# Last feed-forward: three passes of an exact product in one PSUM bank, raised in place by ScalarE

## The chip, the cores and the metric

The kernel runs on one core of one Trainium2 chip. A core has a matrix engine (TensorE, "PE" in the profile, with its weight loads as "PEld"), VectorE ("DVE"), ScalarE ("ACT") and GpSimd ("POOL"), which run side by side, each through its own list of instructions in order, and wait for each other by semaphores. TensorE writes only into PSUM, a small memory of 8 banks of 128 partitions x 512 float32; VectorE and ScalarE read results from there. The metric is the device time of one execution in microseconds (us). Before the change it is 470.54 us, the median of 3 runs (470.39 to 470.64).

## The reference

Two transformer-like layers follow each other over `x` of shape 2 x 512 x 512 (batch, rows, features), each with an attention and a feed-forward part, and a layer norm behind each of the four. Only the last attention and the last feed-forward matter here:

```python
qkv = jnp.einsum('bsc,cf->bsf', x, Wqkv) + bqkv      # head width 128
attn = jax.nn.softmax(jnp.einsum('bqd,bkd->bqk', q, k) * scale, axis=-1)
out = jnp.einsum('bqk,bkd->bqd', attn, v)
x = _layernorm(x + jnp.einsum('bqd,dc->bqc', out, Wo) + bo)
...
gate = jnp.einsum('bsh,ih->bsi', x, w_gate)          # 1376 hidden units
up = jnp.einsum('bsh,ih->bsi', x, w_up)
inter = jax.nn.silu(gate) * up
x = _layernorm(x + jnp.einsum('bsi,hi->bsh', inter, w_down))
```

All of it is float32, and the feed-forward has to be near to exact float32.

## The kernel before

**An exact product out of three fast passes.** TensorE multiplies two float32 operands in several internal passes, but operands of the narrower type `float32r` in one. The last feed-forward therefore splits each operand into parts whose single-pass products add up to the float32 product. `row_parts` (L820) makes of a block of rows an upper part h (ScalarE, L803), a rest l (VectorE, L824) and a difference d = h - 4096 l (VectorE, L825). `weight_parts` (L812) makes of a block of weights h (ScalarE, L803), a copy multiplied by 4096 called `big` (ScalarE, L809), l = big - 4096 h (VectorE, L817) and d = l - h (VectorE, L818). The products h·h and l·l go to one PSUM bank `pm` ("main"), d·d to another, `pc` ("cross"). The result is (1 + 1/4096)·pm + pc/4096. `sum_up` (L1116) makes it: ScalarE copies pc times 1/4096 to SBUF (L1120), then VectorE adds pm times (1 + 1/4096) to it (L1121).

**Tiling.** The 1376 hidden units are cut into 11 chunks of 128 (the last has 96), which are taken in the order `turn`; j counts them. A step is a pair (b, j) of a batch and a chunk. `up1` (L1144) computes for a step gate and up (a = 0 and 1), each with 3 x 4 matmuls of 128 x 128 by 128 x 512, the cross pass first; then come `sum_up` for gate, SiLU on ScalarE (L1163), `sum_up` for up, and their product on VectorE (L1165). The first chunk (j = 0) runs differently: gate and up side by side, and block by block of the 512 features in the order h, l, d, so that it can start while the row parts are still being made. The chunk of 96 has a form of its own (`up1_joined`, L1124), in which half of up is packed behind gate. The steps run (0,0), (0,1), (0,2), (1,0), (1,1), (1,2), then j = 3 to 8 for both batches in turn, then (0,9), (0,10), (1,9), (1,10). Behind step (0,1) the rows of batch 1 are transposed on TensorE (L1042) and split.

**The down products.** `down1` (L1188) handles one tile of 128 rows: 11 cross matmuls into `pdc`, 22 main matmuls into `pdm`, and two additions on VectorE (L1205) that multiply each bank by its factor and add it to `x`; then statistics (L1208, L1214), 1/standard deviation on GpSimd (L145, L146), an offset on GpSimd (L1000), the scaling on ScalarE (`scalar_norm`, L1001) and the store. There are 8 tiles; the last is cut into two halves of 256 columns, each with its own banks, and its norm is finished by VectorE and ScalarE together (L1220 to L1226).

**What sets the order.** The kernel is written in program order; a scheduler orders the instructions of TensorE, VectorE and ScalarE from it, GpSimd's stay as written, and `issue_after` in the source ties some. Splitting weights for later chunks (`split_up`, `split_down`) has no PE work of its own, and the scheduler puts it where the engines seem to have room. Space for the parts comes from a list `free` of SBUF pieces that are done with; an instruction that writes into a reused piece waits for its last reader.

**Ahead of it, the end of the attention.** For batch 1: `values` (L982) multiplies by the probabilities in two halves of 256 columns (L989); VectorE copies each half out of PSUM (L993), `output` (L1003) multiplies it by `wo1` (L1005), `attended` (L1008) adds it to `x` on VectorE (L1010). Rows of batch 0 are scaled by ScalarE (L1001) and transposed by TensorE (L1042); rows of batch 1 get statistics (L137, L139), GpSimd's L145 and L146, and are scaled by VectorE (L151).

Of the kernel before, what the change touches and what calls it, by code (L numbers as in the profile page):

```python
# [10 lines left out]
F32 = mybir.dt.float32  # L11
# [8 lines left out]
P = 128  # L20
# [18 lines left out]
def kernel(  # L39
# [754 lines left out]

    BIG = 4096.0
    MAIN, CROSS = 1.0 + 1.0 / BIG, 1.0 / BIG
    UPPER = 1.0 - 2.0**-13
    cutp = ctx.enter_context(tc.tile_pool(name="cutp", bufs=2))  # L800

    def upper(h, src):
        return nc.scalar.activation(h, src, AF.Copy, scale=UPPER)  # L803

    def weight_upper(w, h, name):

        upper(h, w)
        big = cutp.tile([P, 512], F32, tag="big", name=f"big_{name}")
        nc.scalar.activation(big, w, AF.Copy, scale=BIG)  # L809
        return big  # L810

    def weight_parts(w, parts, name, big=None):  # L812

        h, l, d = parts
        if big is None:
            big = weight_upper(w, h, name)
        nc.vector.scalar_tensor_tensor(l, h.bitcast(F32), -BIG, big, ALU.mult, ALU.add)  # L817
        return nc.vector.tensor_sub(d, l.bitcast(F32), h.bitcast(F32))  # L818

    def row_parts(src, parts):  # L820

# [18 lines left out]
        del free[:n]  # L840
        return got

    def split_up(j, room, bigs=(None, None)):

        c = turn[j]
        n = CHUNKS[c][1]
        for a in range(2):
            up_parts[j, a] = room[3 * a : 3 * a + 3]
            if n == P:
                w = gus[c][:, a].rearrange("p k i -> p (k i)")  # L850
            else:
                w = gus[c][a]
            if n == P or a == 0:
                done = weight_parts(w, up_parts[j, a], f"gu{j}_{a}", bigs[a])
                continue

            u, w = (v.rearrange("p (k i) -> p k i", k=NK) for v in (up_parts[j, a][0], w))
            h = u[:, :, : P // 2]
            upper(h, w)
            done = nc.vector.tensor_sub(u[:, :, P // 2 :], w, h.bitcast(F32))  # L860
        own = wffn.tile([P, 2 * n // P, 512], F32R, tag=f"gu{c}", name=f"ugu_{c}")
        free.extend(units(own))
        return done
# [49 lines left out]

    room2 = room1[6:] + take(4)
    with tc.issue_after(moved.ins):
        bigs2 = [
            weight_upper(
                gus[turn[2]][:, a].rearrange("p k i -> p (k i)"), room2[3 * a], f"gu2_{a}"
            )
            for a in range(2)  # L920
        ]

    probs = []

# [46 lines left out]
    moved = exponentials(1, got1, {1: copies[-4], 2: copies[-2]})  # L971
    table(AF.Silu, moved)
    with tc.issue_after(scaled_max.ins):
        done = split_up(2, room2, bigs2)
    with tc.issue_after(done.ins):
        for _, sums in probs:
            nc.vector.reciprocal(sums, sums)
# [106 lines left out]

    evicted = [fp.tile([P, S], F32, tag="sg", name=f"ev_{i}") for i in range(2)]
    for i in range(2):
        evicted += units(query_tile(f"ev_q{i}"))

    def products(b, j, a):


        h, l, d = (u.rearrange("p (k i) -> p k i", k=NK) for u in up_parts[j, a])
        pc, pm = psum(f"pc_{b}_{j}_{a}"), psum(f"pm_{b}_{j}_{a}")
        passes = [
            [(w[:, k], x3[b][k][i], (pm, pm, pc)[i]) for i, w in enumerate((h, l, d))]
            for k in range(NK)
        ]
        return pc, pm, passes

    def run(passes, by_block):  # L1100

        if by_block:
            todo = [p for block in passes for p in block]
        else:
            todo = [block[i] for i in (2, 0, 1) for block in passes]
        begun = {}
        for _, _, p in todo:
            begun[id(p)] = begun.get(id(p), 0) + 1
        left = dict(begun)
        for w, x, p in todo:  # L1110
            nc.tensor.matmul(  # L1111
                p, w, x, start=(left[id(p)] == begun[id(p)]), stop=(left[id(p)] == 1)
            )
            left[id(p)] -= 1

    def sum_up(pc, pm):  # L1116

        ev = evicted.pop(0)
        evicted.append(ev)
        nc.scalar.activation(ev, pc, AF.Copy, scale=CROSS)  # L1120
        nc.vector.scalar_tensor_tensor(ev, pm, MAIN, ev, ALU.mult, ALU.add)  # L1121
        return ev

    def up1_joined(b, j, it):  # L1124

        n = CHUNKS[turn[j]][1]
        pc, pm, passes = products(b, j, 0)
        run(passes, False)
        u = up_parts[j, 1][0].rearrange("p (k i) -> p k i", k=NK)
        p = psum(f"pm_{b}_{j}_1")  # L1130
        run([[(u[:, k], x3[b][k][i], p) for i in range(2)] for k in range(NK)], True)
        both = sum_up(pc, pm)
        moved = nc.scalar.activation(both[:n], both[:n], AF.Silu)
        wide = evicted.pop(0)
        evicted.append(wide)
        nc.scalar.copy(wide[: P // 2], p[P // 2 :])
        nc.scalar.copy(wide[P // 2 : n], both[n:])
        nc.vector.tensor_add(wide[: P // 2], wide[: P // 2], p[: P // 2])
        nc.vector.tensor_mul(it, both[:n], wide[:n])
        return moved  # L1140

    its = {}

    def up1(b, j):  # L1144

        n = CHUNKS[turn[j]][1]
        g = j // 4
        if (b, g) not in its:
            its[b, g] = fp.tile(
                [P, GROUPS[g], S], F32, tag=f"it{b}{g}", name=f"it_f1{b}{g}", bufs=1  # L1150
            )
            if g == turn.index(last) // 4:
                nc.gpsimd.memset(its[b, g][96:, turn.index(last) % 4, :], 0.0)
        if n < P:
            return up1_joined(b, j, its[b, g][:n, j % 4, :])
        (pc0, pm0, passes0), (pc1, pm1, passes1) = (products(b, j, a) for a in range(2))
        if j == 0:
            run([[x for y in zip(p, q) for x in y] for p, q in zip(passes0, passes1)], True)
        else:
            run(passes0, False)  # L1160
            run(passes1, False)
        gate = sum_up(pc0, pm0)
        moved = nc.scalar.activation(gate, gate, AF.Silu)  # L1163
        wide = sum_up(pc1, pm1)
        nc.vector.tensor_mul(its[b, g][:n, j % 4, :], gate, wide)  # L1165
        return moved

    down_parts = []

    def split_down():  # L1170
        c = turn[len(down_parts)]
        parts = take(3)
        weight_parts(wds[c], parts, f"wd{c}")
        down_parts.append(parts)
        free.append(wdp.tile([P, 512], F32R, tag=f"wd{c}", name=f"uwd_{c}"))

# [8 lines left out]
            got.append((room, parts))  # L1185
        return got

    def down1(b, t, got, cuts):  # L1188

        x = xs[b][t]  # L1190
        w = HID // cuts
        st = small.tile([P, cuts, 6], F32, tag=f"st{cuts}", name=f"st_{b}_{t}")
        for i in range(cuts):
            cols = slice(i * w, (i + 1) * w)
            pc, pm = psum(f"pdc_{b}_{t}_{i}"), psum(f"pdm_{b}_{t}_{i}")
            for p, kinds in ((pc, (2,)), (pm, (0, 1))):
                for j in range(len(turn)):
                    for kind in kinds:
                        nc.tensor.matmul(  # L1199
                            p[:, :w], got[j // 4][1][kind][:, j % 4], down_parts[j][kind][:, cols],  # L1200
                            start=(j == 0 and kind == kinds[0]),
                            stop=(j == last and kind == kinds[-1]),
                        )
            for p, f in ((pc, CROSS), (pm, MAIN)):
                nc.vector.scalar_tensor_tensor(  # L1205
                    x[:, cols], p[:, :w], f, x[:, cols], ALU.mult, ALU.add
                )
            nc.vector.bn_stats(st[:, i, :], x[:, cols])  # L1208
            if i == 0 and cuts > 1:

# [17 lines left out]
            free.extend(room)  # L1228

    free.extend(units(const.tile([P, 3, 512], F32R, tag="wqkv", name="u_wqkv")))  # L1230
    for tag in ("wo1", "bo"):
        free.append(const.tile([P, 512], F32R, tag=tag, name=f"u_{tag}"))

# [1 line left out]
    steps += [(b, j) for j in range(3, last - 1) for b in range(B)]  # L1235
    steps += [(0, last - 1), (0, last), (1, last - 1), (1, last)]
    ahead = 3
    for i, (b, j) in enumerate(steps):
        before, moved = moved, up1(b, j)
        if i == 1:  # L1240
            rooms[1] = rows_room(1, "r1")
            x3[1], _ = split_rows(1, rooms[1])
        if b == 1 and j not in (0, 1, 3, 6):

            kept = 2 if j == 2 else 0
            free.extend((up_parts[j, 0] + up_parts[j, 1])[kept:])
        if (b, j) == (0, last):
            free.extend(rooms[0])
        if (b, j) == (1, last):
            free.extend(rooms[1])  # L1250
        with tc.issue_after(before.ins):
            if ahead <= last and b == 1:
                split_up(
                    ahead, room0 if ahead in (3, 6) else take(6 if turn[ahead] < last else 4)
                )
# [6 lines left out]

    while len(down_parts) <= last:
        split_down()
    quarters.append(split_tile(0, 1))
    for i, (b, t) in enumerate(order):
        down1(b, t, quarters[i], 2 if i == len(order) - 1 else 1)
        if i + 2 < len(order):
            quarters.append(split_tile(*order[i + 2]))


# [49 lines left out]
```

## Time and profile before

| | |
|---|---|
| median of 3 runs | 470.54 us |
| span of the profiled execution, first to last instruction | 468.7 us |
| mean granted clock of TensorE | 0.998 |
| VectorE, whole span | 329.5 us in 627 instructions |
| ScalarE, whole span | 267.5 us in 507 instructions |
| GpSimd, whole span | 115.1 us in 144 instructions |
| L1120, ScalarE, pc times 1/4096 | 42 instructions, 0.59 us each |
| L1121, VectorE, pm added | 42 instructions, 0.69 us each |
| L809, ScalarE, `big` | 32 instructions, 0.62 us each |
| L1205, VectorE, down sums | 18 instructions, 0.69 us each (0.42 us for 256 columns) |

The profile shows one execution. Its page has no total for that execution, only the span; the median of the runs is 1.84 us above it, which is what lies before the first and behind the last instruction. An instruction's duration includes its latency, so that instructions of one engine overlap a little in the records; where instructions stand back to back the distance between their starts is their price.

### The profile page before, as it was taken

Reading aid. Unit: us, or ns where it says so; the run is one execution under the profiler, and the core shown is the slowest. Engines: PE = TensorE matmul, PEld = TensorE weight load, DVE = VectorE, ACT = ScalarE, POOL = GpSimd, SP = SyncE. Lnnn points to the kernel's source line nnn. Section 1 sums busy time; section 2 is a strip of 40 time slices with the busy share of each in tenths; the row PEclk is TensorE's granted clock in tenths of the full one; section 3 lists DMA queues with packets and bytes.
Section 4 is the critical chain, followed back from the end, with each engine's and each line's share of the span. In section 5 each row is a group of like instructions: output and inputs, shape, how many; then the busy total and the mean of one; then the engine's idle time right before and its main releaser. Section 6 shows DMA issues by size and latency. Waiting matters only on the chain.

```text
span 468.7 us, 5727 instructions
## 1 busy us (share of the span) xinstructions
PE 461.0 (98%) x1883; PEld 329.0 (70%) x1883; DVE 329.5 (70%) x627; ACT 267.5 (57%) x507; POOL 115.1 (25%) x144
## 2 busy tenths in 40 slices
PE   9999999999999999999999999999999999999994
PEld 8454444434478888888866567888888888888884
DVE  1165677767876767775979889895755778998632
ACT  3344799557756767456756842584645768443101
POOL 0235101566543053600357032000000000050111
PEclk9999999999999999999999999999999999999999
DMA  8989900000006500051390000000000000001001
GB/s 284 381 297 363 387 9 0 0 0 3 1 1 134 201 1 3 11 162 45 91 390 31 0 1 1 1 0 1 1 0 1 0 1 1 1 24 45 37 31 45
DMA packets 21651, 35.02 MB, mean 75 GB/s; under 512 B 9840, under 2 KB 10736, under 8 KB 21616
## 3 DMA queue, kind: packets, MB, share of 16 engines
q1 hardware_dynamic: 19616, 33.73, 20.7%
q10 hardware_dynamic: 1872, 0.56, 0.5%
q8 instruction: 22, 0.36, 0.3%
q0 software_dynamic: 128, 0.26, 0.3%
q14 instruction: 13, 0.11, 0.1%
HBM read 31.40 MB, written 2.10 MB: 71 GB/s over the span
## 4 chain that ended last, share of the span: by engine, by line
PE 71%; ACT 7%; DVE 5%; issue 3%; POOL 0%; POOLq 0%; DVEq 0%; ACTq 0%
PE pm L1111 17%; PE pg_f L611 9%; PE pu_f L611 9%; PE pc L1111 8%; PE pdm L1199 7%; PE pd_f L666 4%; PE pdc L1199 4%; DVE x L450 3%; PE pqk L893 3%; PE po L428 2%; ACT y L441 2%; ACT t L463 2%; PE pv L906 2%; PE pot L989 1%; PE po L1005 1%
## 5 line engine op out<-in xcount | busy, mean ns | idle before, releaser
L428 PE MATMUL po<-mw,q 128*128 128x512 f32 x128 | 57.1, 598 | 0.3 <-DVE mv_a L139 0.2
L352 PE MATMUL pq<-xt_a,wq 128*128 128x512 f32 (+1 forms) x152 | 56.9, 526 | 0.0
L145 POOL TENSOR_TENSOR rstd_f<-mv_f,ln_eps 128x1 f32<-128x1 f32 x15 | 4.4, 293 | 169.3 <-DVE mv_f L1214 130.2
L428 PEld LDWEIGHTS po<-mw,q 128*128 128x128 f32 x128 | 22.9, 189 | 32.1 <-issue 17.7
L352 PEld LDWEIGHTS pq<-xt_a,wq 128*128 128x128 f32 x152 | 26.2, 190 | 27.4 <-issue 25.7
L1111 PE MATMUL pm<-r,ugu 128*128 128x512 f32 x152 | 37.7, 389 | 0.0
L1111 PE MATMUL pm<-r,it_early 128*128 128x512 f32 x144 | 36.7, 392 | 0.0
L1111 PEld LDWEIGHTS pm<-r,ugu 128*128 128x128 f32 x152 | 28.5, 188 | 5.9
L1111 PEld LDWEIGHTS pm<-r,it_early 128*128 128x128 f32 x144 | 27.0, 188 | 6.1 <-issue 0.5
L169 ACT ACTIVATE ta_f<-y_f,below_half 128x512 int8<-128x512 f32 (+1 forms) x22 | 15.9, 721 | 27.0 <-DVE y_f L157 26.7
L450 DVE SCALAR_TENSOR_TENSOR x<-po,den,x 128x511 f32<-128x511 f32 x40 | 29.8, 745 | 1.9
L1121 DVE SCALAR_TENSOR_TENSOR ev_q<-pm,ev_q 128x512 f32<-128x512 f32 x27 | 18.6, 688 | 14.4 <-PE pm L1111 14.4
L637 DVE SCALAR_TENSOR_TENSOR it_f<-tb_f,ta_f 128x512 fp32r<-128x512 int16 (+1 forms) x22 | 15.4, 702 | 18.3 <-ACT tb_f L170 18.3
L445 POOL TENSOR_TENSOR y<-y,y 128x511 f32<-128x511 f32 x16 | 20.3, 1271 | 31.5 <-ACT y L441 30.8
L388 ACT ACTIVATE e<-pq,bq 128x512 f32<-128x512 f32 x16 | 11.1, 692 | 24.1 <-PE pq L352 20.6
L611 PE MATMUL pg_f<-xh,tu 128*128 128x512 f32 x88 | 24.3, 398 | 0.0
L1120 ACT ACTIVATE ev_q<-pc 128x512 f32<-128x512 f32 x27 | 16.0, 593 | 14.2 <-PE pc L1111 14.1
L465 POOL TENSOR_SCALAR td<-wd,inv_down 128x512 fp32r<-128x512 f32 x11 | 18.2, 1668 | 22.1 <-DVE inv_down L205 22.1
L611 PE MATMUL pg_f<-xl,tu 128*128 128x512 f32 x88 | 23.6, 390 | 0.0
L611 PE MATMUL pu_f<-xh,tu 128*128 128x512 f32 x88 | 23.5, 389 | 0.0
L611 PE MATMUL pu_f<-xl,tu 128*128 128x512 f32 x88 | 23.5, 389 | 0.0
L1001 ACT ACTIVATE x<-x,off_f,rstd_f 128x512 f32<-128x512 f32 x7 | 5.7, 816 | 27.7 <-POOL off_f L1000 27.7
(315 smaller groups left out, 1087.5 us busy)
## 6 DMA issues: line engine op xcount, KB each, us to landing
gu<-in_gu SPq DMA_DIRECT2D x20, 512.0 KB, 7.9
wo<-in_wo SPq DMA_DIRECT2D x16, 512.0 KB, 6.9
wd<-in_wd SPq DMA_DIRECT2D x20, 256.0 KB, 4.5
wq<-in_wq SPq DMA_DIRECT2D x8, 256.0 KB, 4.9
x<-in_x SPq DMA_DIRECT2D x7, 256.0 KB, 5.4
out<-x SPq DMA_DIRECT2D x7, 256.0 KB, 2.0
wqkv<-in_wqkv SPq DMA_DIRECT2D x1, 768.0 KB, 10.8
xt_f<-squares SPq DMA_DIRECT2D x9, 64.0 KB, 2.4
```

The costliest lines, as they stand in the source:

```text
L169: nc.scalar.activation(a[:n], y, AF.Relu, bias=below_half[:n])
L352: done = nc.tensor.matmul(pq[:, at], wq[h][:, k, :], xt[:, k, at], start=(k == 0), stop=(k == NK - 1),)
L428: nc.tensor.matmul(po, qs[b][h0 + j][:, ts(t, P)], mw[:, h0 + j, :], start=True, stop=True,)
L445: nc.gpsimd.tensor_add(ys[0][:, :LAST], ys[0][:, :LAST], y[:, :LAST])
L450: steps.append(nc.vector.scalar_tensor_tensor(x[:, :LAST], four[j][:, :LAST], d, x[:, :LAST], ALU.mult, ALU.add))
L465: eng.tensor_scalar(out, w, factor, None, ALU.mult)
L611: nc.tensor.matmul(pp[a], t[:, a, i % NK, :], x2[b][i], start=(i == 0), stop=(i == 2 * NK - 1),)
L666: nc.tensor.matmul(pd, inter[b][c][:, ts(t, P)], td[c].bitcast(F32R), start=(c == 0), stop=(c == last),)
L1111: nc.tensor.matmul(p, w, x, start=(left[id(p)] == begun[id(p)]), stop=(left[id(p)] == 1))
L1120: nc.scalar.activation(ev, pc, AF.Copy, scale=CROSS)
L1121: nc.vector.scalar_tensor_tensor(ev, pm, MAIN, ev, ALU.mult, ALU.add)
L1199: nc.tensor.matmul(p[:, :w], got[j // 4][1][kind][:, j % 4], down_parts[j][kind][:, cols], start=(j == 0 and kind == kinds[0]), stop=(j == ...
```

## The change

The three passes of a product now use one bank `p`. The main passes g·h and l·l add up in it, where g is the weight's upper part divided by 4096 already. ScalarE then multiplies the bank in place by 4097 (`raise_main`), and the cross pass d·d adds to the bank with `start=False`. The bank then holds the finished product. `big` is no longer made: l = w - 4096 g comes from the weight itself.

The cross pass of a product is issued one step later than its main passes: a step runs the main passes of its gate, the cross pass of the previous step's gate, the main passes of its up, and the cross pass of the previous step's up. In the same way a down tile's cross pass follows the next tile's main passes. SiLU and the multiplication behind it, and the VectorE addition behind a down tile, read the finished bank. What follows a step (freeing of pieces, splitting of later weights) moves one step back with it. Four pieces of SBUF that held evicted results, and the two that held `big`, go to `free`.

```diff
+    def upper(h, src, scale=UPPER):
+        return nc.scalar.activation(h, src, AF.Copy, scale=scale)
+    def weight_upper(w, g):
+        return upper(g, w, UPPER / BIG)
-        big = cutp.tile([P, 512], F32, tag="big", name=f"big_{name}")
-        nc.scalar.activation(big, w, AF.Copy, scale=BIG)
-        nc.vector.scalar_tensor_tensor(l, h.bitcast(F32), -BIG, big, ALU.mult, ALU.add)
+        nc.vector.scalar_tensor_tensor(l, g.bitcast(F32), -BIG, w, ALU.mult, ALU.add)
...
+    def raise_main(p):
+        return nc.scalar.activation(p, p, AF.Copy, scale=BIG + 1.0)
...
     for i in range(2):
-        evicted += units(query_tile(f"ev_q{i}"))
+        free.extend(units(wqp.tile([P, 2, 512], F32R, tag="wq", name=f"u_q{i}")))
...
-        nc.scalar.activation(ev, pc, AF.Copy, scale=CROSS)
-        nc.vector.scalar_tensor_tensor(ev, pm, MAIN, ev, ALU.mult, ALU.add)
+    def main(job):
+        p, (g, l, _) = job
+        run(p, g + l)
+        raise_main(p)
+    def cross(job):
+        p, (_, _, d) = job
+        run(p, d, False)
...
+    def up1(b, j, held):
+        it, jobs = up1_begin(b, j)
+        late = held[3] if held else []
+        half = None
+        for i in range(2):
+            if i == len(jobs):
+                half = up1_half(b, j)
+            elif j > 0:
+                main(jobs[i])
+            if i < len(late):
+                cross(late[i])
+        return (b, j, it, jobs, half)
...
     for i, (b, t) in enumerate(order):
-        down1(b, t, quarters[i], 2 if i == len(order) - 1 else 1)
+        jobs = down1_begin(b, t, quarters[i], 2 if i == len(order) - 1 else 1)
+        main(jobs[0])
+        if i == 0:
+            for job in held[3]:
+                cross(job)
+            finish_up()
+            quarters.append(split_tile(0, 1))
+        else:
+            down1_finish(*begun)
+        for job in jobs[1:]:
+            main(job)
+        begun = (b, t, quarters[i], jobs)
...
+    down1_finish(*begun)
```

`up1_begin` issues, for j = 0, the main passes of gate and up block by block and then the two `raise_main`. `down1_finish` runs `cross` for each bank of a tile, adds the bank to `x` with one `tensor_add`, and goes on with statistics, norm and store as before.

## The prediction

> **What bounds the kernel now.** I read the busy shares first, then the chain of waits in order of time through the last feed-forward, then the timeline at three places. Busy time, whole page:
>
> ```profile
> PE 461.0 (98%) x1883; PEld 329.0 (70%) x1883; DVE 329.5 (70%) x627; ACT 267.5 (57%) x507; POOL 115.1 (25%) x144
> ```
>
> A busy PE alone proves little, so the chain from 276 to 300 us (start, us, what, matmuls):
>
> ```profile
> 277.19 2.58 PE po L1005 x6
> 279.76 1.75 PE pt_f L1042 x16
> 281.51 0.86 PE po L1005 x2
> 282.37 0.93 PE pm L1111 x4
> 283.30 0.47 PE pc L1111 x2
> 283.76 0.92 PE pm L1111 x4
> ...
> 291.48 1.82 PE pm L1111 x8
> 293.31 1.75 PE pt_f L1042 x16
> ```
>
> Each piece begins where the one before ends, and a 512-column matmul takes 0.227 us (1.82/8). Counting confirms it to the end: the up products are 520 matmuls, 117.9 us, plus one round of transposes, 1.75 us; from 282.26 (the first, by starts) this gives 401.9, and the chain shows the first down matmul at 402.08. Seven down tiles of 33 at 0.227 and 66 at 0.12 give 60.3 us: 462.2, where the last ends. So TensorE never waits from the end of the attention on, and nothing taken from another engine can shorten this stretch. Only waits can be added, or the 6 us behind the last matmul changed.
>
> **What the skill says.** "PSUM — Partial Sum Buffer", The four PSUM rules: writes of ScalarE leave the bits that decide between adding and overwriting alone. The main passes have set them, so the cross pass adds; the change does what it says. No trace of before has such a write. "Perfetto Trace Analysis", Identifying the Most-Contended Engine: matmul busy time is a poor measure of TensorE. That agrees: 98% is reported in the attention too; the count above carries the argument. "ScalarE: Activation LUTs", What ACT_TABLE_LOAD costs: about 186 ns plus 0.833 ns per column with immediate scale; the trace has 593 ns for 512 columns out of PSUM (L1120), and I use the trace.
>
> **The change part by part.** TensorE: the same 1883 matmuls. VectorE: 42 additions L1121 and half of L1205 (9) go, 51 x 0.69 = 35 us. ScalarE: 42 of L1120 and 32 of L809 go, 51 multiplications come, 23 fewer x 0.6 = 14 us. None is on the path, so all this is worth 0.
>
> The multiplication in place isn't in the trace. Bounds: L1120's 0.59 us, or 0.2 less if a store to PSUM is quicker (the section Step-by-step of the ScalarE page calls it faster; no run here shows it), or twice that. In the up stage it is ready after its 8 main matmuls and needed 24 matmuls later, 5.4 us; in the down stage 33 later, 7.5 us. At most four other ScalarE instructions stand between two multiplications in the up stage, seven at the first down tile. Hidden at any of these values. Each cross pass also waits for it, but a satisfied wait costs nothing visible: steps before have such waits and hold 0.227 us.
>
> What remains is where the order moves something late. In the instruction order of the changed program I find three places.
>
> *Place A, end of the attention.* The freed pieces let the scheduler begin splitting down weights early: one split (ScalarE upper, VectorE L817- and L818-like) now stands between the copies of the transposed probabilities of batch 1, the VectorE list also puts the statistics of batch 0's fourth tile ahead of the first half's copy of L993. Before:
>
> ```profile
> 276.03 0.39 DVE L993 COPY ot<-pot 128x256 f32<-128x256 f32 x1
> 276.34 0.68 DVE L137 BATCH_NORM_STATS2 st_a<-x 128x6 f32<-128x512 f32 x1
> 277.02 2.74 PE L1005 MATMUL po<-wo,ot 128*128 128x512 f32 x6
> ```
>
> The copy has 277.02 - 276.42 = 0.6 us to spare. After, from ScalarE's upper ending at 269.21 (it follows the table load, 268.59 + 0.62), with VectorE starts 0.60 to 0.65 apart as in this stretch: split 269.25, copy 269.85, split 270.46, copy 271.06, two additions 271.67 and 272.32, two statistics 272.97 and 273.57, aggregate and addition 274.25, aggregate and addition 274.98, two statistics 275.62 and 276.22, aggregate 276.82, copy 276.91, done 277.30. A TensorE that stood starts some 0.15 us after its releaser (a VectorE end at 118.50, its matmul at 118.65). So 277.45 for 277.02: **+0.43 us** (0.3 to 0.6). The rows of batch 0 come later too, 280.24 for the fourth, and are needed at 280.36: no further wait.
>
> *Place B, second batch's rows.* Step (0,0) runs 16 main matmuls, (0,1) 16, and only the cross pass of (0,0), 8, before the transposes; before it was 48. They are reached 8 x 0.227 = 1.81 us earlier against the rows:
>
> ```profile
> 291.87 0.55 DVE L151 TENSOR_SCALAR x<-x,mv_a,rstd_a 128x512 f32<-128x512 f32 x1 [0.44 <-POOL rstd_a L146]
> 293.14 1.91 PE L1042 MATMUL pt_f<-ident,x 128*128 128x128 f32 x16
> ```
>
> The fourth row tile is ready at 292.42 and was needed by the fourth transpose, 293.14 + 0.33 = 293.47. The VectorE and GpSimd list between is unchanged; it moves with place A. So needed at 291.66, ready and released at 292.57: **+0.9 us** (0.7 to 1.1). A wait inside step (0,0), where l of a block is now needed sooner (0.1 at most), would only be taken from this. What the split of these rows feeds is 24 matmuls later, 5.4 us, for eight 0.6 us instructions: covered.
>
> *Place C, the end.* On ScalarE, the multiplication of the last half tile stands behind the norm of the tile before (L1001). That norm's chain before:
>
> ```profile
> 454.28 0.28 PE L1199 MATMUL pdc<-u_wqkv,ugu 128*128 128x256 f32 x1
> 454.48 0.69 DVE L1205 SCALAR_TENSOR_TENSOR x<-pdm,x 128x512 f32<-128x512 f32 x1 [4.29 <-PE pdm L1199]
> 457.61 0.81 ACT L1001 ACTIVATE x<-x,off_f,rstd_f 128x512 f32<-128x512 f32 x1 [6.86 <-POOL off_f L1000]
> ```
>
> With T the end of that tile's cross pass: addition T + 0.20, statistics + 0.73, aggregate + 0.73 (as at 440.94 and 441.67), GpSimd and ScalarE + 1.48, norm over at T + 3.95, multiplication of 256 columns (0.38) at T + 4.25, TensorE at T + 4.4. Its list: 22 main matmuls x 0.12 = 2.64, 11 of the other half's cross pass 1.32, so it stands from T + 3.96: **+0.44 us** (0.3 to 0.6). Behind TensorE the last addition reads one bank as before (0.42 us), so the 6 us stay. The store of the tile before starts some 4 us later than now, but ahead of the last stores; 0.
>
> Transition from up to down: the parts of the first tile are made one step later; l of its third group is ready about 1 us before its matmul. 0.
>
> Sum: 0.43 + 0.9 + 0.44 = 1.77; span 468.7 becomes 470.5, and with the same 1.84 around it 472.3 us.
>
> **Rivals.** 0.2% of 470.54 is 0.94 us; less can't be told from no change. (1) *Rows in time, no change:* place B alone decides. If batch 1's rows are ready 0.75 us sooner than the 292.42 plus A says, 0.9 goes to 0.15 and the sum is 1.0 or less, 471.4. For it: GpSimd's four L146 there take 0.55 to 0.85, and at 0.55 each the chain is 0.5 shorter; durations there are rough. Against: same list, same neighbours. (2) *A price on each cross pass:* if each of the 51 cross passes costs 0.05 us to restart, 2.5 more, 474.8. Against: satisfied waits are free before. For: nothing before adds onto a bank that ScalarE wrote. (3) *ScalarE becomes late:* a multiplication behind a queued split or SiLU that waits long; it needs over 5 us, and would cost perhaps 0.5 in some steps: 474. (4) *Faster:* would need a gap in TensorE's stretch; I see none. It would come out at 469.5 at best, if the freed engines let the tail behind TensorE run 1 us shorter.
>
> **How the numbers follow.** Forecast as worked 0.72; rival 1 0.10; rivals 2 and 3 together 0.13; faster 0.05. The three bounds give 1.3 to 2.3, 471.8 to 472.8; to hold 8 in 10 I reach half into rival 1 and the smaller prices of 2 and 3: 471.2 to 473.6. Slower by over 0.2%: 0.72 + 0.13 = 0.85; same 0.10; faster 0.05.
>
> **What would show it.** A: idle before L1005's `po` of about 0.4 us released by VectorE's copy. B: about 0.9 us before the second transposes, released by the row scaling. C: about 0.4 us before the last 11 matmuls, released by ScalarE. Between them 0.227 us per matmul without gaps, and no gap before cross passes in the steps. Gaps there, or a shorter stretch behind the last matmul, would prove me wrong.

## The result and the profile after

The changed kernel takes 472.50 us (median of 4 runs, 471.83 to 472.83) against 470.47 us for the kernel before (4 runs): a ratio of 1.0043, 95% interval 1.0029 to 1.0057. It is slower, by 2.0 us. In the text below the ratio is always the comparison's own, with its interval; it is not the quotient of the two medians.

The first part of the page of the changed kernel and, from its groups of instructions, the new one (busy us, mean ns of one, then idle time ahead of it and what ended it):

```profile
PE 461.5 (98%) x1883; PEld 328.3 (70%) x1883; DVE 300.5 (64%) x576; ACT 255.2 (54%) x484; POOL 114.0 (24%) x144
...
L818 ACT ACTIVATE pu<-pu 128x512 f32<-128x512 f32 x42 | 24.3, 582 | 49.3 <-PE pu L1096 40.5
```

VectorE has 51 instructions and 29 us fewer, ScalarE 23 instructions and 12 us fewer, TensorE the same 1883 matmuls and the same busy share. The multiplication in place takes 0.582 us for 512 columns. The time went up although no engine does more; so it must be in waits of TensorE, and its timeline shows where. Changed kernel, TensorE, from the last attention products to the steps behind the second transposes (start, us, engine, line, operation, count, wait and releaser):

```profile
273.00 3.62 PE L985 MATMUL pot<-xt_p,v 128*128 128x256 f32 x16
276.61 2.84 PE L1001 MATMUL po<-wo,ot 128*128 128x512 f32 x6
279.29 0.49 PE L1038 MATMUL pt_f<-ident,x 128*128 128x128 f32 x3
280.23 1.64 PE L1038 MATMUL pt_f<-ident,x 128*128 128x128 f32 x13 [0.45 <-ACT x L997]
281.70 1.02 PE L1001 MATMUL po<-wo,ot 128*128 128x512 f32 x2
282.16 2.88 PE L1138 MATMUL pu<-r,it_early 128*128 128x512 f32 x10
...
291.91 2.25 PE L1038 MATMUL pt_f<-ident,x 128*128 128x128 f32 x16
293.92 2.98 PE L1096 MATMUL pu<-r,it_early 128*128 128x512 f32 x12
```

Kernel before, the same view at the same places (its row of the second transposes, 293.14, stands in the prediction):

```profile
273.57 3.62 PE L989 MATMUL pot<-xt_p,v 128*128 128x256 f32 x16
...
281.80 1.50 PE L1111 MATMUL pm<-r,it_early 128*128 128x512 f32 x4
...
294.81 1.17 PE L1111 MATMUL pc<-r,ugu 128*128 128x512 f32 x4
```

Three readings, each a difference of starts, so that a start of the whole program that lies earlier or later drops out:

- *Place A.* From the first of the half products (273.00) to the first up matmul (282.16): 9.16 us. Before, 273.57 to 281.80: 8.23. Lost: 0.93.
- *The first step.* From there to the second transposes (291.91): 9.75 us for 40 matmuls. Before, 281.80 to 293.14 for 48; without eight of 0.227 that is 9.52. Lost: 0.23.
- *Place B.* From the first of these transposes to the matmul behind them: 2.01 us against 1.67 before (293.14 to 294.81). Lost: 0.34.

From here to the last tile nothing is lost. The first down matmul in the TensorE timelines, changed kernel and kernel before:

```profile
401.00 0.39 PE L1096 MATMUL pd<-ugu,r 128*128 128x512 f32 x1
...
401.92 0.39 PE L1199 MATMUL pdc<-u_wqkv,uwd 128*128 128x512 f32 x1
```

Between 293.92 and 401.00 lie 472 up matmuls, 107.08 us; the kernel before has 472 between 294.81 and 401.92, 107.11 us. So a cross pass that adds onto a bank multiplied by ScalarE costs TensorE nothing that shows here. The last wait is in the last tile (changed kernel, timeline of VectorE, ScalarE and the one TensorE row with a wait):

```profile
458.03 0.69 DVE L1229 TENSOR_TENSOR x<-x,pd 128x512 f32<-128x512 f32 x1 [3.52 <-PE pd L1096]
...
460.97 0.81 ACT L997 ACTIVATE x<-x,off_f,rstd_f 128x512 f32<-128x512 f32 x1 [4.07 <-POOL off_f L996]
461.69 0.36 ACT L818 ACTIVATE pd<-pd 128x256 f32<-128x256 f32 x1
...
462.10 0.51 PE L1096 MATMUL pd<-u_q,r 128*128 128x256 f32 x2 [0.16 <-ACT pd L818]
...
463.71 0.42 DVE L1229 TENSOR_TENSOR x<-x,pd 128x256 f32<-128x256 f32 x1 [0.66 <-PE pd L1096]
```

The last row in the kernel before is:

```profile
462.39 0.42 DVE L1205 SCALAR_TENSOR_TENSOR x<-pdm,x 128x256 f32<-128x256 f32 x1 [2.21 <-PE pdm L1199]
```

*Place C.* The multiplication of the last half tile (461.69) begins when the norm ahead of it on ScalarE ends, and the last 11 cross matmuls wait for it. The first and the last addition shown for the changed kernel lie 5.68 us apart; in runs below without this wait they lie 5.27 apart. Lost: 0.41, more than the 0.16 of idle time in the view, which counts from the end of the matmul ahead and not from where the next one would have started. The tail behind the last addition is as long as before (463.71 to the end of the span 6.3 us, before 462.39 to 468.7 also 6.3).

The sum is 0.93 + 0.23 + 0.34 + 0.41 = 1.91 us, and the medians differ by 2.03. Nothing of size is left over: from the first half product to the last addition it is 190.71 us (273.00 to 463.71), before 188.82 (273.57 to 462.39), 1.89 more. The two spans differ by only 1.3 us (470.0 and 468.7), because this profiled execution began its first long products 0.57 us sooner (5.58 against 6.15), long before any changed instruction, and kept that lead to the end of the attention. Compared by spans alone the change would have looked a third cheaper than it is.

### The profile page after: what moved, and what is told of

It is laid out like the page before. It is cut to its first block, busy times and chain, and to the rows that moved or that the text cites. A ratio compares the mean times of both kernels' runs of the same rounds, so it can differ in the third digit from the quotient of the medians.

```text
span 470.0 us, 5618 instructions
## 1 busy us (share of the span) xinstructions
PE 461.5 (98%) x1883; PEld 328.3 (70%) x1883; DVE 300.5 (64%) x576; ACT 255.2 (54%) x484; POOL 114.0 (24%) x144
## 4 chain that ended last, share of the span: by engine, by line
PE 66%; ACT 9%; DVE 7%; issue 4%; POOL 2%; POOLq 0%; DVEq 0%; ACTq 0%
PE pu L1096 22%; PE pd L1096 12%; PE pg_f L611 9%; PE pu_f L611 8%; PE pd_f L666 4%; DVE x L450 3%; PE pqk L893 3%; PE po L428 2%; ACT y L441 2%; ACT t L463 2%; PE pv L906 2%; PE psc L927 1%; ACT den L432 1%; DVE st_a L137 1%; PE pt_a L127 1%
## 5 line engine op out<-in xcount | busy, mean ns | idle before, releaser
L1096 PE MATMUL pu<-r,ugu 128*128 128x512 f32 x224 | 53.9, 389 | 0.0
L818 ACT ACTIVATE pu<-pu 128x512 f32<-128x512 f32 x42 | 24.3, 582 | 49.3 <-PE pu L1096 40.5
L1096 PEld LDWEIGHTS pu<-r,ugu 128*128 128x128 f32 x224 | 42.0, 188 | 8.7
L145 POOL TENSOR_TENSOR rstd_f<-mv_f,ln_eps 128x1 f32<-128x1 f32 x15 | 5.9, 395 | 172.5 <-DVE mv_f L1236 133.5
L1096 PE MATMUL pu<-r,it_early 128*128 128x512 f32 x176 | 42.6, 390 | 0.0
L1096 PEld LDWEIGHTS pu<-r,it_early 128*128 128x128 f32 x176 | 33.0, 188 | 6.9
L1152 DVE TENSOR_TENSOR it_f<-ev,pu 128x512 f32<-128x512 f32 x20 | 13.7, 684 | 24.8 <-PE pu L1096 24.8
```

What stands on the lines that cost most here:

```text
L818: return nc.scalar.activation(p, p, AF.Copy, scale=BIG + 1.0)
L1096: nc.tensor.matmul(p, w, x, start=(start and i == 0), stop=(i == n - 1), skip_group_check=not start,)
```

## The experiments

All runs together, "lost" being read as above in the one profiled execution of each (A, first step, B, C), in us:

| run | median | ratio to before, interval | A | first step | B | C | sum |
|---|---|---|---|---|---|---|---|
| changed kernel | 472.50 | 1.0043, 1.0029 to 1.0057 | 0.93 | 0.23 | 0.34 | 0.41 | 1.91 |
| a_split_later | 471.78 | 1.0022, 1.0015 to 1.0030 | 0.01 | 0.23 | 0.34 | 0.41 | 0.99 |
| b_rows_8_later | 472.12 | 1.0030, 1.0021 to 1.0039 | 0.93 | 0.22 | 0 | 0.41 | 1.56 |
| c_raise_first | 472.32 | 1.0035, 1.0022 to 1.0048 | 0.94 | 0.21 | 0.35 | 0 | 1.50 |
| abc_together | 470.71 | 1.0000, 0.9992 to 1.0008 | 0 | 0.23 | 0 | 0 | 0.23 |
| a_one_split | 471.66 | 1.0020, 1.0014 to 1.0027 | 0.28 | 0.25 | 0.32 | 0.41 | 1.26 |
| abc_low_first | 470.56 | 0.9998, 0.9990 to 1.0006 | 0.01 | -0.03 | 0 | 0 | 0 |
| abc_raise_twice | 470.99 | 1.0006, 0.9997 to 1.0014 | 0.01 | 0.39 | 0 | 0 | 0.40 |
| abc_vector_back | 472.59 | 1.0032, 1.0019 to 1.0045 | 0.01 | 0.21 | 0.75 | 0.87 | 1.84 |
| vector_back_middle | 470.58 | 0.9998, 0.9991 to 1.0004 | 0.01 | -0.01 | 0 | 0 | 0 |

In these runs the kernel before had medians of 470.57 to 470.70. In every row 1 plus the sum divided by 470.6 lies in the interval.

**Each place undone alone.** The prediction said that the three places are waits made by the order of instructions. The rival was that each of the 51 cross passes pays a small price, and that the waits are only what one sees of it. Place A:

```diff
-            for _ in range(2):
+            for _ in range(2 if i else 0):
                 if len(down_parts) <= last and len(free) >= (9 if ahead <= last else 3):
                     split_down()
```

> Place A alone undone: no down weights are split in the first step, so VectorE's list from the probabilities of batch 1 to the scaling of batch 1's rows is that of the kernel before again. Theory (three late places; A and B hang on the same VectorE list): the 0.93 us that the profile shows lost between 273 and 282 us goes, but the second transposes are then reached 0.93 us sooner while their rows come only 0.62 sooner, so the wait ahead of them grows from about 0.56 to about 0.9 us. Net -0.6: 471.9 us. If the places were independent, as the prediction added them: -0.93, 471.6, with the wait ahead of the second transposes still 0.56. Rival (a price on each of the 51 cross passes, 0.04 us each, and the waits only its symptoms): no change, 472.5.

VectorE's list up to the rows of batch 1 is then that of the kernel before. Its TensorE timeline:

```profile
281.28 2.84 PE L1138 MATMUL pu<-r,it_early 128*128 128x512 f32 x10
...
291.03 2.25 PE L1038 MATMUL pt_f<-ident,x 128*128 128x128 f32 x16
293.04 3.01 PE L1096 MATMUL pu<-r,it_early 128*128 128x512 f32 x12
```

A is gone (273.04 to 281.28, 8.24 us), and B is what it was: 291.03 to 293.04, 2.01 us. So my expectation that B would grow was wrong. The places simply add, as the prediction had them: the statistics of batch 1's rows stand on VectorE behind the split of batch 0's rows, which itself waits for the transposes, so a delay at A moves rows and TensorE alike.

Place B, where the call that transposes and splits batch 1's rows moves from behind the second step to behind the first main pass of the third:

```diff
-        if i == 1:
-            rooms[1] = rows_room(1, "r1")
-            x3[1], _ = split_rows(1, rooms[1])
...
                 main(jobs[i])
+            if rows and i == 0:
+                rows()
             if i < len(late):
                 cross(late[i])
```

> Place B alone undone: the second batch's transposes come 8 matmuls (1.81 us) later, behind the first main pass of the third step, so that 48 up matmuls stand ahead of them as in the kernel before. Theory: the 0.56 us of waiting inside these 16 transposes goes, they take 1.75 us in one piece, and nothing else waits, since 16 matmuls (3.6 us) still stand between them and the first product of batch 1: -0.56, 471.9 us. It fails if the wait turns up in front of the first product of batch 1. Rival (price per cross pass): no change, 472.5.

Its TensorE timeline at the second transposes:

```profile
294.44 1.91 PE L1038 MATMUL pt_f<-ident,x 128*128 128x128 f32 x16
296.11 1.17 PE L1096 MATMUL pu<-r,it_early 128*128 128x512 f32 x4
```

The transposes take 1.67 us, in one piece, and no wait turns up behind them. Only 0.34 us are gained in the trace and not 0.56: the rest of what I had put down to B is lost earlier, inside the first step, where this edit changes nothing.

This run also shows how firm the rows' own time is. The third of GpSimd's four L146 for them (1/standard deviation), in the kernel before, the changed kernel and this run:

```profile
290.00 0.85 POOL L146 TENSOR_TENSOR rstd_a<-rstd_a,minus_half 128x1 f32<-128x1 f32 x1
...
290.35 0.55 POOL L146 TENSOR_TENSOR rstd_a<-rstd_a,minus_half 128x1 f32<-128x1 f32 x1
...
291.08 0.85 POOL L146 TENSOR_TENSOR rstd_a<-rstd_a,minus_half 128x1 f32<-128x1 f32 x1
```

The lists of VectorE and GpSimd up to here are the changed kernel's. Each time L146 starts some 0.1 us behind the second of VectorE's scalings (L151). Of the eleven profiles of this document seven have 0.55 and four 0.84 or 0.85, and in nanoseconds the traces separate them: in the seven it starts 97 to 101 ns behind the scaling, in the four 103 to 108. The kernel before is one of the four, the changed kernel one of the seven, but b_rows_8_later falls among the four with the changed kernel's lists. So a few nanoseconds decide over 0.30 us of B in a single profile; by what mechanism, no run shows.

Place C, where the norm of the tile before is tied behind the multiplication of the last half tile:

```diff
-            scalar_norm(x, root(mv, f"f1_{b}_{t}"), f"f1_{b}_{t}")
+        raised = [main(job) for job in between]
+            scalar_norm(x, root(mv, f"f1_{b}_{t}"), f"f1_{b}_{t}", raised)
```

> Place C alone undone: on ScalarE the multiplication of the last half tile goes ahead of the norm of the tile before; no other list changes. Theory: the last 11 cross matmuls follow without a wait, and the end of the last matmul comes 0.40 us sooner against the end of the tile before: -0.4, 472.1 us. The store of the tile before starts some 0.3 us later and hides behind the last stores. Rival (price per cross pass): no change, 472.5.

ScalarE's two instructions have changed places (this kernel's norm is L1000), and the additions that were 5.68 us apart are 5.27 apart, 457.81 to 463.08. Its ScalarE timeline:

```profile
460.44 0.37 ACT L818 ACTIVATE pd<-pd 128x256 f32<-128x256 f32 x1 [3.77 <-PE pd L1099]
460.74 0.81 ACT L1000 ACTIVATE x<-x,off_f,rstd_f 128x512 f32<-128x512 f32 x1
```

The median alone, with five runs, tells little (0.2 us less than the changed kernel, where 0.4 were expected); here the trace decides.

**All three edits.**

> All three edits. Theory: with the three places gone TensorE has no gap from the end of the attention on, and the last feed-forward takes as long as in the kernel before, with 51 VectorE and 23 ScalarE instructions fewer that are worth nothing: 470.5 us, within 0.3 of the kernel before. Rival (a price of 0.04 us on each of 51 cross passes): still about 2 us above the kernel before, 472.4. Rival (freed engines shorten the tail): below 470.2.

The ratio is 1.0000 (0.9992 to 1.0008). The 51 multiplications and cross passes are all still there, so a price for each of 0.04 us, 2 us in all, is excluded: the interval leaves 0.4 us at most for all 51. What remains is 0.23 us in the first step. The weight loads' waits in this kernel name one cause there, `PEld pu L1141 <- DVE r L824`, 0.3 us once.

**What place A is made of.** In the changed kernel 0.16 of the 0.93 us are lost ahead of the first `po` matmul, 0.10 in the `po` matmuls, and 0.67 inside the first transposes, which wait for ScalarE's norm of batch 0's fourth row tile. That norm hangs on GpSimd. Changed kernel, timeline of VectorE, GpSimd and ScalarE:

```profile
276.33 0.19 POOL L145 TENSOR_TENSOR rstd_a<-mv_a,ln_eps 128x1 f32<-128x1 f32 x1 [0.33 <-DVE mv_a L139]
...
276.99 0.68 DVE L814 SCALAR_TENSOR_TENSOR u_q<-u_q,wd 128x512 fp32r<-128x512 f32 x1
277.25 0.56 POOL L996 TENSOR_SCALAR off_a<-mv_a,rstd_a 128x1 f32<-128x1 f32 x1
...
278.51 0.68 DVE L815 TENSOR_TENSOR u_q<-u_q,u_q 128x512 fp32r<-128x512 f32 x1
278.68 0.65 POOL L996 TENSOR_SCALAR off_a<-mv_a,rstd_a 128x1 f32<-128x1 f32 x1
...
279.36 0.81 ACT L997 ACTIVATE x<-x,off_a,rstd_a 128x512 f32<-128x512 f32 x1 [0.71 <-POOL off_a L996]
```

The view of the same line by its instructions (ns: least, median, most), in the kernel before:

```profile
L1000 POOL TENSOR_SCALAR off_a<-mv_a,rstd_a x4: 264/264/265, 274.5 to 278.7; 128x1 f32<-128x1 f32 x4
```

Two of the four take more than twice as long after the change, and both run beside a VectorE instruction of the early weight split, each ending 0.14 us behind it. The Trainium skill, "SBUF — State Buffer", section Who interferes with whom, says that a VectorE instruction with two inputs in SBUF contends with a GpSimd instruction that reads SBUF, and that the later of the two waits until the first has ended. L814 and L815 have both inputs in SBUF, and the trace agrees; the additions L1010 of the kernel before, one of whose inputs is in PSUM, ran beside the last of its four without effect (0.26 us). To test it, only the second of the two early splits is held back:

```diff
-            for _ in range(2):
+            for _ in range(2 if i else 1):
```

> The changed kernel, but only one down weight is split in the first step instead of two: the VectorE pieces of the second split (L814 and L815 into u_q, at 276.99 and 278.51 in the changed kernel) and its ScalarE part go to the next step; the lists are otherwise the same. In the changed kernel GpSimd's L996 took 0.56 and 0.65 us where these two ran, and 0.26 elsewhere, and the norm of batch 0's fourth row tile, which the first transposes wait for, hangs on it. Theory (the second split's VectorE work holds up GpSimd's chain): both L996 take 0.26, the norm ends by 0.7 us sooner, the 0.67 us lost inside the first transposes goes, only the 0.2 to 0.3 us ahead of them stay: A from 0.93 to about 0.25, 471.8 us. Rival (A is only the length of VectorE's list, which is displaced half as much): A about 0.45 to 0.5 and a wait for the norm still there, 472.1.

The same view of this run:

```profile
L996 POOL TENSOR_SCALAR off_a<-mv_a,rstd_a x4: 264/266/266, 274.8 to 278.6; 128x1 f32<-128x1 f32 x4
```

And its TensorE timeline at the first transposes:

```profile
279.49 1.91 PE L1038 MATMUL pt_f<-ident,x 128*128 128x128 f32 x16
281.24 1.02 PE L1001 MATMUL po<-wo,ot 128*128 128x512 f32 x2
```

GpSimd's four are short again, the 16 transposes run in one piece, and A falls from 0.93 to 0.28. Half the split was two thirds of the loss. Taking it away removes both its place in VectorE's list and its hold on GpSimd, but the traces separate the two. GpSimd's row for the third row tile in this run:

```profile
276.54 0.19 POOL L145 TENSOR_TENSOR rstd_a<-mv_a,ln_eps 128x1 f32<-128x1 f32 x1 [0.32 <-DVE mv_a L139]
```

It waits for VectorE's aggregate (L139) and starts 3.35 us behind the first half product (273.19 in this run); in the changed kernel it is 3.33 (276.33 behind 273.00). So VectorE delivered equally late in both. From there to the start of the fourth tile's norm GpSimd's chain takes 3.03 us in the changed kernel (to 279.36) and 2.35 here (to 278.89): the 0.68 between them are the two longer L996. What this edit leaves, 0.28 us, goes only when the first split is put off too (a_split_later).

**What the first step lacks.** The chain of waits with all three edits (L1141: main passes of the first step; L1099: the next step's, which the scheduler puts between them):

```profile
282.15 2.31 PE pu L1141 x10
284.46 0.23 PE pu L1099
284.69 1.10 PE pu L1141 x4
285.79 0.46 PE pu L1099 x2
286.25 0.46 PE pu L1141 x2
```

Before, a block of 128 features gave TensorE six matmuls (1.36 us) before it asked for the next block's parts, now four (0.91), the d parts being asked for only in the cross pass. VectorE still made l and d of a block in turn. The edit makes the four l first:

```diff
+            done = row_parts(pts[k][0], parts[k], bool(behind))
...
+        if behind:
+            for k in range(NK):
+                with tc.issue_after(done.ins):
+                    rest = row_rest(parts[k])
```

> All three edits, and for batch 0's rows VectorE makes the second parts of all four blocks (L824) before the third parts (L825), which only the cross pass needs. With the three edits the first up step still takes 0.23 us longer than in the kernel before up to the second transposes, and the weight load of a product of L1138 is released by L824 there. Theory (main passes alone ask for a block's second part every 4 matmuls instead of every 6): the 0.23 us go, 470.5 us, and up start to second transposes is 11.3 us as in the kernel before. If something else holds that step, no change: 470.7. A difference of 0.2 us is at the edge of what the times tell, so the trace decides.

The chain of waits of this run:

```profile
281.85 3.65 PE pu L1152 x16
285.50 7.26 PE pu L1110 x32
292.76 1.75 PE pt_f L1047 x16
```

The step's 16 main matmuls now run in one piece and the 0.23 us are gone in the trace; the time (0.9998, 0.9990 to 1.0006) can't tell so small a step. With it all four losses are undone, and the new scheme takes just the time of the old one: no version that I ran beats the kernel before.

**What the freed engines are worth.** The prediction put 35 us of VectorE and 14 us of ScalarE at nothing. Three runs give work back on top of the edits. ScalarE:

```diff
     def raise_main(p):
+        nc.scalar.activation(p, p, AF.Copy)
         return nc.scalar.activation(p, p, AF.Copy, scale=BIG + 1.0)
```

> All three edits, and each of the 51 accumulators is rewritten twice by ScalarE: copied in place, then multiplied, so that the step between main and cross pass takes about 1.16 instead of 0.58 us and ScalarE has 51 instructions (some 29 us) more. Theory (hidden: 5.4 us of cover in the up stage, 7.5 in the down stage, 1.3 at the last half tile): no change to the kernel with the three edits, 470.7 us, within 0.2. Rival (each cross pass pays for the step ahead of it): at least 0.05 us each, 2.5 in all, 473.2; if only the last half tile's cover is too short, +0.4.

26 us more of ScalarE (281.3 busy), and 470.99, ratio 1.0006 (0.9997 to 1.0014). The trace loses 0.16 us more in the first step and nothing elsewhere. The timelines of ScalarE and of the weight loads show what it is (L818 copies, L819 multiplies):

```profile
286.60 1.07 ACT L818 ACTIVATE pu<-pu 128x512 f32<-128x512 f32 x2 [4.50 <-PE pu L1142]
287.57 1.08 ACT L819 ACTIVATE pu<-pu 128x512 f32<-128x512 f32 x2
288.21 4.86 PEld L1100 LDWEIGHTS pu<-r,it_early 128*128 128x128 f32 x22 [0.32 <-ACT pu L819]
```

In the first step the banks of gate and up are complete together. ScalarE copies both before it multiplies the first, so that this one is finished only 1.6 us after its copy began, and the first step's cross pass, seven matmuls behind the last main matmul, waits for it. Everywhere else the doubled work is hidden. VectorE:

```diff
     def raise_main(p):
-        return nc.scalar.activation(p, p, AF.Copy, scale=BIG + 1.0)
+        nc.scalar.activation(p, p, AF.Copy, scale=BIG + 1.0)
+        return nc.vector.tensor_copy(p, p)
```

> All three edits, and VectorE gets back as many instructions as the change took from it: each of the 51 accumulators is copied in place by VectorE behind ScalarE's multiplication, about 0.6 us each, some 30 us in all. Theory (what was taken from VectorE is worth nothing here): 470.7 us, within 0.3 of the kernel with the three edits; only the last half tile, whose cover is 1.3 us, may add up to 0.2. Rival (the freed VectorE shortens something that the waits took back): slower by over 0.5, 471.3 or more.

That expectation failed: the gain of the three edits is lost again. Its TensorE timeline shows that it is lost in two places:

```profile
292.12 1.18 PE L1042 MATMUL pt_f<-ident,x 128*128 128x128 f32 x6
293.36 2.15 PE L1100 MATMUL pu<-r,it_early 128*128 128x512 f32 x8
295.35 1.25 PE L1042 MATMUL pt_f<-ident,x 128*128 128x128 f32 x10
...
463.24 0.50 PE L1100 MATMUL pd<-u_q,r 128*128 128x256 f32 x2 [0.63 <-DVE pd L819]
```

The added copies made the scheduler put the first of the second transposes back to where they wait for the rows (0.75 us there), and in the last tile ScalarE's multiplication is behind the norm again (462.35 and 461.63), because the tie now names the copy, with the copy on top (0.87). So the run didn't test what it was made for. The next adds 37 of the 51 copies, on top of the kernel with the l parts first, and leaves both places alone. With two accumulators to a step, the first that is copied (number 12, counted from 0) belongs to the seventh step of the up stage, not to the fourth as the expectation says:

```diff
+        if 12 <= len(raised_so_far) < 49:
+            nc.vector.tensor_copy(p, p)
+        raised_so_far.append(p)
```

> The kernel with the three edits and the second parts first, and VectorE copies an accumulator in place behind ScalarE's multiplication as in the run with all 51 copies, but only for 37 of them, from the fourth step of the up stage to the seventh tile of the down stage; around the second batch's transposes and in the last tile nothing is added, and TensorE's order stays as it was. 37 x 0.65 = 24 us of VectorE work. Theory (VectorE's time is worth nothing where TensorE has cover, and the run with all copies was slow from its two tight places alone): 470.6 us, within 0.3 of the kernel without copies, no wait of TensorE. Rival (VectorE's load as such costs, 1.9 us for 51 copies): 1.4 us for 37, 472.0.

The busy line of its page:

```profile
PE 460.6 (98%) x1883; PEld 328.7 (70%) x1883; DVE 321.9 (69%) x613; ACT 255.7 (55%) x484; POOL 113.8 (24%) x144
```

24 us more of VectorE (298.3 without), and no change: 470.58 us, 0.9998 (0.9991 to 1.0004), with no wait of TensorE. VectorE's time is worth nothing there; the order of the lists at the two tight places is what the run with all copies paid for.

## Why the prediction was right, and where it was off

- *The bound.* TensorE from the end of the attention on, counted by matmuls: right. 472 up matmuls take 107.08 us after and 107.11 before; saved work on the other engines brought nothing, and given back to VectorE between the tight places it cost nothing. Two figures of that count need care: 282.26 is not a start that the view shows (the first up matmul is recorded at 281.80, while the one ahead of it still runs), and 402.08 is the chain's, 0.16 behind the timeline's 401.92.
- *The multiplication in place.* 0.4 to 1.2 us, hidden: right, 0.58. The cover of 24 matmuls, 5.4 us, is too long for the first step, where it is seven matmuls, 1.6 us; at 0.58 this is still enough, and abc_raise_twice lost 0.16 us there.
- *The sum.* 1.77 us was forecast, 1.91 is in the trace, 2.03 in the medians. That is closer than its terms deserve.
- *Place A, +0.43 (0.3 to 0.6).* Too small: 0.93. The early split of down weights was the cause named, and a_split_later shows it. The step that failed is "The rows of batch 0 come later too, 280.24 for the fourth, and are needed at 280.36: no further wait." It has no term for GpSimd's L996, which took 0.26 us before and 0.56 and 0.65 beside the split, so that the norm ended 0.55 us after it was needed (280.17 against 279.62). The wait for VectorE's copy, which I held for the whole of A, is 0.16 us, with 0.10 behind it.
- *The first step.* "0.1 at most" and "taken from" B: 0.23 us, undone in the trace by abc_low_first. It was indeed taken from B.
- *Place B, +0.9 (0.7 to 1.1).* Too large: 0.34. Of the difference, 0.23 is the first step's. Another 0.30 is the time from the first statistics to the end of the last scaling of these rows: 286.71 to 292.42, 5.71 us, before, and 287.06 to 292.47, 5.41, after. So 0.9 - 0.30 - 0.23 = 0.37. "The VectorE and GpSimd list between is unchanged; it moves with place A" holds for the list: the statistics begin 4.91 us behind the first up matmul before and 4.90 after. What failed is taking its length from one profile: the third L146 took 0.85 us there and 0.55 in the changed kernel, and b_rows_8_later shows that this is not the change's doing. With 0.85 the changed kernel would have lost about 0.64 at B (an estimate, 0.34 + 0.30), against 0.9 - 0.23 = 0.67. The first rival's doubt, that these durations are rough, is borne out in part.
- *Place C, +0.44.* Right: 0.41. The norm ended at 461.78; with T at 457.83, 0.20 ahead of the addition, the prediction has T + 3.95 = 461.78.
- *The rivals.* A price of 0.04 us for each cross pass is excluded by abc_together, and so is a late ScalarE in the steps: of the changed kernel's matmuls only those of place C wait for the multiplication. The faster case needed a shorter tail; it is as long as before.

The middle of the forecast came out so close because A's error (0.50 too small) and that of B with the first step (0.57 for 0.9, 0.33 too large) nearly cancel, and that is luck; the range would have held with either error alone (472.8 or 472.0). A's error came from taking GpSimd's durations as fixed although VectorE's work beside them changed, the first step's from the order in which its matmuls ask for the row parts, and B's for the most part from a duration that differs from one profile to the next.

## What to carry to other kernels

Where one engine is back to back, as TensorE is here, saved work on the others is worth nothing, and the order that the change brings along decides: freed buffers let a scheduler start later work early, and passes that are put off bring what follows forward to where it isn't ready. Look for such places in the instruction lists, and read each as a difference of starts in both traces, since spans carry the chance of the start (0.57 us here). A term read from one profile carries such a chance too (0.30 us for one GpSimd instruction here): look at the same instruction in several profiles. When a VectorE instruction moves beside a chain of small GpSimd instructions, take the chain at its contended price, not at the one in the profile.

## What the runs showed of the hardware

- A GpSimd instruction on 128 x 1 elements took 0.26 us beside VectorE additions that read PSUM, and 0.56 and 0.65 us beside VectorE instructions with both inputs in SBUF; without those, 0.26 again.
- GpSimd's `pow` on 128 x 1 elements (L146, the third for batch 1's rows) took 0.55 us in the seven profiles where it started 97 to 101 ns behind VectorE's scaling L151, and 0.84 or 0.85 in the four where it started 103 to 108 ns behind it.
- A float32 product of 128 x 128 by 128 x 512 (L1005 in the kernel before) stands in the trace as two records with starts 0.43 us apart, some 0.86 us in all; a product of two `float32r` parts is one record, 0.227 us.
- ScalarE multiplied 128 x 512 float32 in place in PSUM in 0.582 us, 128 x 256 in 0.363; the same from PSUM to SBUF took 0.593 in the kernel before. The Trainium skill, "ScalarE: Activation LUTs", section Step-by-step, calls the store to PSUM the faster one; here that is 0.011 us, not the 0.2 that the prediction allowed for. Matmuls that then add to the bank keep the step of 0.227 us (107.08 us for 472).
